# A message-passing layer on one core: a split first group, ten supertiles gathered from 128 rows, a last pass in units of four bins, and an early flag

## The chip, the cores and the metric

The kernel runs on one core of a Trainium2 chip. The core has five engines with an instruction stream each: PE (TensorE, matmuls and weight loads), DVE (VectorE), ACT (ScalarE), POOL (GpSimd) and SP (SyncE, which here only issues DMAs). They share the SBUF and sixteen DMA engines. The metric is device time in microseconds (us) of one execution.

## The reference, cut to what matters

There are N = 12,500 nodes with 128 features and E = 400,000 edges, sorted by `dst`. With `src` as the index to sum over, `dst` as the index to gather from and `rcut` the edge weight, the layer computes:

```
h    = relu(layernorm(x)) @ W_in2f.T                       # 12500 x 128
W    = smu(f_ij @ W_f1.T + b_f1) @ W_f2.T + b_f2           # 400000 x 128, f_ij has 20 columns
msg  = h[dst] * (W * rcut[:, None])                        # one message per edge
agg  = segment_sum(msg, src, 12500)                        # src is random
out  = x + smu(agg @ W_o1.T + b_o1) @ W_o2.T + b_o2
```

`smu` is a smooth activation that the kernel makes of a Gelu and a multiple of its input. `h[dst]` is a gather with neighbouring edges close together; the sum over `src` is a scatter to random rows.

## The kernel before, in words

**Edges.** The edges lie in 3125 tiles of 128. Four tiles are a group (GRP), two groups a supertile (SUP = 8 tiles), so there are 391 supertiles and 782 groups. For each group the main loop makes the messages in this chain: `hide` (PE, L625: filter layer 1), `bend` (ACT, L633: Gelu), `smooth` (DVE, L641), `weigh` (PE, L678: filter layer 2), `gather` (PE, L657 or L659: h[dst] as a product with a one-hot matrix), `take` (ACT, L667: copy out of PSUM), `mix` (DVE, L688), `turn` (PE, L699: four transposes), `send` (ACT, L712 and L715: times the weight, into a message tile `ms`), and `scatter` (POOL, L726): one indirect DMA for each tile of 128 messages, which writes each message into a slot of its own in DRAM. The slot comes from a count: `bins` (DVE, L556, four instructions), `count` (PE, L570 to L573), `read` (DVE, L600) and `number` (DVE, L612). The program order on each engine is written out by hand, and each engine runs its own list in that order.

**One-hot matrix.** Usually the edges of a group look at a window of 42 rows of h, loaded as three bf16 parts (126 partitions); the one-hot `oh` is made on ACT by two instructions a group (`pick_part`, L523 and L524). The first FEW tiles (6 supertiles, so 12 groups) look at the first 128 rows of h instead: `pick` makes the one-hot on DVE (L507), and the gather takes three matmuls (L657) in place of one.

**Epochs and bins.** The nodes are 98 bins of 128. The supertiles are split into ten epochs of 59, 59, 59, 59, 48, 37, 27, 20, 16 and 7. In an epoch every bin has a region of slots in DRAM, of Q blocks of 128 rows (Q is 6 in the first epochs, 2 in the ninth, 1 in the tenth). While an epoch is scattered, `parts` works through the (bin, block) pairs of the epoch before: `fetch` (SP, L757) loads 12 blocks into a tile `rw` (four buffers), `choose` (DVE, L771) makes a selection matrix `se`, `add` (PE, L787) multiplies, and DVE adds the sum to `agg` (L800), 98 x 128 columns. The messages of the last two epochs are made early and kept in DRAM; at the end of the program a short loop only loads and scatters them. In that loop LEFT = 36 of the 196 pairs of the ninth epoch are held back until the last scatter is issued.

**Opening.** Before the loop stands a hand-ordered opening: loads of x, w and the first indices; layernorm and h of the first bin; the one-hot, count and messages of group 0 as a whole; constants in between. `quiet_ends` has POOL clear a tile `zero`, with which the slot regions are cleared by DMA (`clear`, L187 and L191), and fill buffers; it waits for DVE. The list `opening` holds 14 steps (the rest of the first 512 tiles' indices, and h of bins 1 to 3), one of which runs at each of the three `step()` calls of a group. After it come the `steps` that prepare all other nodes and indices, spread over the first epoch by the expression `taken_steps * 3 * (eps_of[0][1] * PER - 15) < slot * COUNT`.

**Last pass.** After the last scatter the rest of the ninth epoch is added, then the tenth: nine fetches of 12 bins (the first of two bins), and for each unit of four bins Gelu (ACT, L1132), a sum (POOL, L1138), the last product (PE, L279), the residual (DVE, L283) and a DMA to `out` (SP, L285). Then a count of violated assumptions (`bad`) is summed over the partitions by a matmul (L1189), loaded by every engine into a register (`values_load`, L1194), and an `If` (L1195) branches over a general path that the inputs do not need. It holds some 270 DMA issues of SP.

Of the kernel before, what the change touches and what calls it, by code (L numbers as in the profile page):

```python
# [9 lines left out]
F32 = mybir.dt.float32  # L10
# [9 lines left out]
P = 128  # L20
# [8 lines left out]
SUP = 8  # L29
# [13 lines left out]
def gnn_kernel(  # L43
# [46 lines left out]
    for a, n in eps_of:  # L90
# [21 lines left out]
    make_identity(nc, ident)  # L112
# [3 lines left out]
    nc.vector.memset(ones1, 1.0)  # L116
# [4 lines left out]
    nc.vector.tensor_scalar(prow, pcol, float(WIN), -float(WIN), op0=ALU.is_ge, op1=ALU.mult)  # L121
    nc.vector.tensor_add(prow, prow, pcol)
    late = const.tile([P, 1], F32, name="late")
    nc.vector.tensor_scalar(late, pcol, float(2 * WIN), -float(WIN), op0=ALU.is_ge, op1=ALU.mult)
    nc.vector.tensor_add(prow, prow, late)
    nrow = const.tile([P, 1], F32, name="nrow")
    nc.vector.tensor_scalar(nrow, prow, -1.0, None, op0=ALU.mult)
    irow = const.tile([P, P], F32, name="irow")
    nc.gpsimd.iota(irow, pattern=[[1, P]], base=0, channel_multiplier=0,
                   allow_small_or_imprecise_dtypes=True)  # L130

# [6 lines left out]
    def counting_constants():  # L138
        nc.vector.tensor_scalar(lift, ident, BIG, None, op0=ALU.mult)
        nc.vector.scalar_tensor_tensor(tri, irow, pcol, lift, op0=ALU.is_gt, op1=ALU.add)  # L140
        nc.vector.memset(ones_h, 1.0)
        nc.vector.tensor_sub(rest_h, ones_h, tri)
        nc.vector.memset(none, 0.0)

    onesb = const.tile([P, P], F32, name="onesb")
    nc.vector.memset(onesb, 1.0)
# [8 lines left out]
    nc.vector.memset(bad, 0.0)  # L155

# [51 lines left out]
    def deviations(a, b):  # L208
        nc.scalar.activation(rstd[:, a:b], mv[:, a:b, 1], AF.Sqrt, bias=eps)
        nc.vector.reciprocal(rstd[:, a:b], rstd[:, a:b])  # L210
        nc.vector.scalar_tensor_tensor(down[:, a:b], mv[:, a:b, 0], -1.0, rstd[:, a:b], op0=ALU.mult, op1=ALU.mult)
# [78 lines left out]
    with tc.tile_pool(name="ld", bufs=4) as ld, \  # L290
# [17 lines left out]
        FEW = 6 * SUP  # L308
# [9 lines left out]
        def whole_bins(to, sf, si):  # L318

            nc.vector.tensor_copy(sf, si)  # L320
            nc.vector.tensor_scalar(to, sf, 1.0 / P, -(P - 1) / (2.0 * P), op0=ALU.mult, op1=ALU.add)
# [81 lines left out]
        nc.sync.dma_start(ds, dst_col[:, 0:FEW])  # L403
        nc.scalar.dma_start(x_sb[:, 0:1, :], bin_rows(x, 0, 1))
        nc.sync.dma_start(ss, src_col[:, 0:FEW])
        nc.scalar.dma_start(w_in, w_in_t)
        fill(0, nc.vector)
        fill(1, nc.vector)
        nc.vector.tensor_copy(irow_ps, irow)
        nc.gpsimd.memset(w_f1, 0.0)  # L410
        nc.sync.dma_start(w_f1[0:R, :], w_f1_t)
        nc.sync.dma_start(w_f1[R:R + 1, :], b_f1)
        nc.sync.dma_start(fbufs[0][0:R, :], f_t[:, 0:SUP * P])
        nc.scalar.dma_start(x_sb[:, 1:HEAD, :], bin_rows(x, 1, HEAD - 1))
        nc.scalar.dma_start(w_o1, w_o1_t)
        nc.sync.dma_start(w_f2, w_f2_t)
        nc.sync.dma_start(b2, b_f2.rearrange("o p -> p o"))
        nc.sync.dma_start(w_sb[:, 0:CH], w_col[:, 0:CH])
        one["fetched"]()
        zr = edge.tile([P, 3 * D], BF, name="zr", bufs=1)  # L420

        def quiet_ends():

            for t in (zero, fbufs[2], zr, fbufs[3], x_sb[:, NB - 1, :]):
                nc.vector.memset(t[:, 0:2], 0.0)  # L425
            nc.gpsimd.memset(zero, 0.0)
            clear(0, len(cleans) - 1, nc.gpsimd)
            fill(2, nc.gpsimd)
            nc.gpsimd.memset(zr, 0.0)
            nc.gpsimd.dma_start(h_dram[NB * P:N + P, :], zr[:N + P - NB * P, :])  # L430
            fill(3, nc.gpsimd)
            nc.gpsimd.memset(x_sb[:, NB - 1, :], 0.0)

        spare = const.tile([P, 2], F32, name="spare")
        nc.scalar.activation(spare[:, 0:1], eps, AF.Sqrt)

# [4 lines left out]
        def later_loads():  # L441
            nc.sync.dma_start(w_o2, w_o2_t)
            nc.sync.dma_start(b1, b_o1.rearrange("o p -> p o"))
# [59 lines left out]
        def pick(s):  # L503

            n = sups[s][1] * P
            oh = edge.tile([P, SUP * P], BF, name="oh", bufs=3)
            nc.vector.tensor_scalar(oh[:, :n], loaded[s][1][:, :n], pcol, None, op0=ALU.is_equal)  # L507
            onehot[s] = oh

        def pick_part(g):  # L510
# [4 lines left out]
            if s < FEW // SUP:  # L515
                if i == 0:
                    pick(s)
                return
# [4 lines left out]
            nc.scalar.activation(oh, loaded[s][1][:, o:o + n], AF.Abs, bias=nrow)  # L523
# [94 lines left out]
        def hide(g):  # L618
# [6 lines left out]
            nc.tensor.matmul(pu[:, :n], w_f1, loaded[g // PER][0][:, o:o + n], start=True, stop=True)  # L625
# [95 lines left out]
        def scatter(g, ms):  # L721

            t, n = groups[g]
            k, ix = epoch[g // PER], taken.pop(g)
            for j in range(n):
# [106 lines left out]
        LEFT = 36  # L832

        def few_bins():
            whole_bins(hi_f[:, 0:FEW], ssf, ss)
# [6 lines left out]
        def spread_group(g):  # L842

            pb = bank("pb")
            for j in range(GRP):
                t = g * GRP + j
                nc.tensor.transpose(pb[:, j, :], dsf[:, t:t + 1].to_broadcast([P, P]), ident)
            return pb.rearrange("p j e -> p (j e)")

        def pick_group(g, pb):  # L850
            nc.vector.tensor_scalar(onehot[0][:, g * GRP * P:(g + 1) * GRP * P], pb, pcol, None, op0=ALU.is_equal)
# [3 lines left out]

        nc.vector.tensor_copy(dsf, ds)
        pb0 = spread_group(0)
        pd = ps1.tile([P, GRP * P], F32, name="pw")
        nc.tensor.transpose(pd[:FEW, 0:P], dsf, ident)
        stats(edge, 0)  # L860
        deviations(0, 1)
        few = edge.tile([FEW, P], BF, name="few", bufs=1)
        nc.scalar.activation(few, pd[:FEW, 0:P], AF.Copy)
        nc.sync.dma_start(rel_dram[0, 0:FEW * P].rearrange("(t e) -> t e", e=P), few)
        few_bins()
# [464 lines left out]
```

## Time and profile before

| | |
|---|---|
| median of 3 runs | 4059.88 us (4059.31 to 4063.59) |
| the profiled execution | 4063.85 us, of which its span from first to last instruction 4062.1 us |
| mean granted TensorE clock | 0.968 |
| busy share of the span | PE 86%, DVE 82%, ACT 73%, POOL 75% |
| scatters (L726) | 3125, first at 19.42 us, last at 3991.16 us |
| last DVE work of a store (L283) ends | 4053.57 us |

All durations below are of the profiled execution, counted from the start of its span. Its own time is 3.97 us above the median. A line such as `L726` is a line of the kernel before. In a group line, `x2944 | 2829.0, 961 | 916.0` is the number of instructions, the busy time, the mean ns of one, and the idle time of the engine just before them. POOL's busy time leaves out what lies between two indirect DMAs.

### The profile page before, as it was taken

How to read it: one execution, taken by the hardware profiler on the slowest of the kernel's cores; microseconds unless marked ns; L12 is line 12 of the kernel's file. 1: busy time of each engine (PE TensorE's matmuls, PEld its weight loads, DVE VectorE, ACT ScalarE, POOL GpSimd, SP SyncE). 2: the span in 40 equal slices, each digit the busy share in tenths (PEclk: the TensorE clock that was granted, in tenths of full speed). 3: DMA queues.
4: the chain of work that ended last, by engine and by line, in shares of the span. 5: the costliest groups of instructions: out<-in, count | busy, mean ns of one | idle time of the engine just before them, and what ended most of it. 6: DMA issues, size and time to landing. Idle time of an engine off the chain costs nothing.

```text
span 4062.1 us, 69847 instructions
## 1 busy us (share of the span) xinstructions
PE 3492.8 (86%) x18417; PEld 2246.9 (55%) x18420; DVE 3328.4 (82%) x7355; ACT 2962.7 (73%) x7256; POOL 3042.2 (75%) x3168
## 2 busy tenths in 40 slices
PE   7777777999988999989999979999899979989657
PEld 3334434555555555555555546666566646656547
DVE  8987776888887888878888878888799869988447
ACT  5779986888886888877888877787777767766001
POOL 6777777777777777777777777777777777777775
PEclk9999998999999999999999999999999989999889
DMA  6976666777756565546565646666566657565987
GB/s 193 240 187 182 190 167 197 210 204 204 208 162 180 174 175 173 173 141 181 174 177 172 176 144 181 182 180 189 154 193 195 183 156 203 170 202 170 274 240 226
DMA packets 510392, 759.72 MB, mean 187 GB/s; under 512 B 174949, under 2 KB 313462, under 8 KB 509856
## 3 DMA queue, kind: packets, MB, share of 16 engines
q1 hardware_dynamic: 402416, 535.77, 48.4%
q0 software_dynamic: 100112, 207.06, 15.3%
q10 hardware_dynamic: 7456, 12.35, 0.8%
q8 instruction: 146, 2.39, 0.3%
q14 instruction: 262, 2.15, 0.2%
HBM read 460.77 MB, written 294.11 MB: 186 GB/s over the span
## 4 chain that ended last, share of the span: by engine, by line
PE 41%; DVE 26%; DMA 13%; ACT 9%; issue 6%; POOL 4%; ACTq 0%; SPq 0%; DVEq 0%; POOLq 0%
PE pw L678 13%; DMA buf<-ms,ix 10%; PE pg L787 10%; DVE se L771 9%; PE pu L625 7%; PE pt L699 7%; DVE mt L688 5%; POOL buf L726 4%; DVE sl L600 3%; ACT ms L715 3%; ACT ge L633 2%; DVE sm L641 2%; PE ph L659 2%; DVE so L556 2%; DVE agg L800 2%
## 5 line engine op out<-in xcount | busy, mean ns | idle before, releaser
L726 POOL DMA_INDIRECT buf<-ms,ix x2944 | 2829.0, 961 | 916.0 <-issue 270.6
L787 PEld LDWEIGHTS pg<-se,rw 128*128 128x128 f32 x8232 | 1080.8, 194 | 343.3 <-issue 277.1
L787 PE MATMUL pg<-se,rw 128*128 128x128 f32 x8232 | 1175.7, 282 | 96.4 <-DVE se L771 75.1
L715 ACT ACTIVATE ms<-pt,w_sb 128x128 f32<-128x128 f32 x3125 | 882.2, 363 | 196.8 <-PE pt L699 176.0
L556 DVE SCALAR_TENSOR_TENSOR so<-irow_ps,hi_f,so 128x98 f16<-128x98 f32 x2936 | 929.7, 317 | 78.0
L678 PE MATMUL pw<-sm,w_f 128*128 128x512 f32 x1564 | 884.1, 648 | 47.9 <-DVE sm L641 46.9
L625 PE MATMUL pu<-f,w_f 128*128 128x512 f32 x1564 | 813.6, 602 | 0.0
L633 ACT ACTIVATE ge<-pu 128x512 f32<-128x512 f32 x782 | 468.0, 598 | 443.6 <-PE pu L625 439.4
L771 DVE TENSOR_TENSOR se<-irow_ps,rw 128x1536 f32<-128x1536 f32 (+2 forms) x356 | 602.3, 1692 | 229.5 <-DMA rw<-buf 228.3
L699 PE MATMUL pt<-ident,mt 128*128 128x128 f32 x2944 | 468.9, 282 | 362.7 <-DVE mt L688 361.1
L688 DVE SCALAR_TENSOR_TENSOR mt<-pw,b,hg 128x512 f32<-128x512 f32 x782 | 583.4, 746 | 173.3 <-ACT hg L667 149.8
L641 DVE SCALAR_TENSOR_TENSOR sm<-pu,ge 128x512 f32<-128x512 f32 x782 | 534.2, 683 | 188.2 <-ACT ge L633 182.4
L699 PEld LDWEIGHTS pt<-ident,mt 128*128 128x128 f32 x2944 | 327.6, 142 | 447.2 <-DVE mt L688 444.4
L524 ACT ACTIVATE oh<-oh,onesb 128x512 bf16<-128x512 bf16 x770 | 555.5, 721 | 25.2
L523 ACT ACTIVATE oh<-rbc,nrow 128x512 bf16<-128x512 bf16 x770 | 551.2, 716 | 1.2 <-DMA rbc<-rel_dram 1.2
L667 ACT ACTIVATE hg<-ph 128x512 f32<-128x512 f32 x782 | 472.1, 604 | 99.9 <-PE ph L659 30.3
L600 DVE TENSOR_REDUCE sl<-pc 128x4 f32<-128x392 f32 x782 | 434.5, 556 | 0.0
L678 PEld LDWEIGHTS pw<-sm,w_f 128*128 128x128 f32 x1564 | 236.5, 191 | 161.8 <-DVE sm L641 124.7
L659 PE MATMUL ph<-oh,hw 126*128 126x512 bf16 x770 | 298.2, 387 | 0.0
L625 PEld LDWEIGHTS pu<-f,w_f 128*128 128x128 f32 x1564 | 256.9, 196 | 67.2 <-issue 57.9
L570 PE MATMUL pc<-so,tri 128*128 128x392 f16 x736 | 243.7, 331 | 1.7 <-DVE agg L425 1.7
L572 PEld LDWEIGHTS <-rest_h 128*128 128x128 f16 x781 | 76.7, 98 | 263.6 <-issue 263.6
(192 smaller groups left out, 2002.1 us busy)
## 6 DMA issues: line engine op xcount, KB each, us to landing
rw<-buf SPq DMA_DIRECT2D x300, 774.0 KB
rbc<-rel_dram SPq DMA_DIRECT2D x389, 256.0 KB
buf<-zero SPq DMA_DIRECT2D x146, 387.0 KB
buf<-ms,ix POOLq DMA_INDIRECT x2944
rw<-buf SPq DMA_DIRECT2D x49, 645.0 KB
f<-in_f_t SPq DMA_DIRECT2D x390, 80.0 KB
hw<-h_dram SPq DMA_DIRECT2D x770, 31.5 KB
kept_rows<-ms ACTq DMA_DIRECT2D x45, 258.0 KB
```

Source lines behind the costliest of these rows:

```text
L524: nc.scalar.activation(oh, oh, AF.Relu, scale=-1.0, bias=onesb[:, 0:1])
L556: nc.vector.scalar_tensor_tensor(so[:, j], irow_ps[:, :NB], hi_f[:, t + j:t + j + 1], so[:, j - 1] if j else before, op0=ALU.is_equal, op1 ...
L600: nc.vector.tensor_reduce(sl[:, :n], pc[:, :n], op=ALU.max, axis=AX.X)
L625: nc.tensor.matmul(pu[:, :n], w_f1, loaded[g // PER][0][:, o:o + n], start=True, stop=True)
L641: nc.vector.scalar_tensor_tensor(sm[:, :n], units_of.pop(g)[:, :n], LIN, hidden[g][:, :n], op0=ALU.mult, op1=ALU.add)
L678: nc.tensor.matmul(pw[:, :n], w_f2, hidden.pop(g)[:, :n], start=True, stop=True)
L688: nc.vector.scalar_tensor_tensor(mt[:, :n], pws.pop(g)[:, :n], b2, rows_of.pop(g)[:, :n], op0=ALU.add, op1=ALU.mult)
L699: nc.tensor.transpose(pt[:, j, :], mt[:, j * P:(j + 1) * P], ident)
L715: nc.scalar.activation(ms[:, j, 0:P], pt[:, j], AF.Copy, scale=w_sb[:, t + j:t + j + 1])
L726: i = nc.gpsimd.indirect_dma_start(out=bufs[k][:, :], out_offset=bass.IndirectOffsetOnAxis(ap=ix[:, j:j + 1], axis=0), in_=ms[:, j, :], in ...
L771: nc.vector.tensor_tensor(se[:, a:a + n], own.unsqueeze(1).to_broadcast([P, n, P]), rows_in[c][:, a:a + n, P:P + 1].to_broadcast([P, n, P] ...
L787: nc.tensor.matmul(pgs[0][:, g, :], rows_in[c][:, o, 0:P], sel[c][:, o, :], start=(q == 0), stop=(q == Q[k] - 1))
```

## The change

1. **First group.** Group 0 is made as its first tile alone (`one_cut`, 128 columns) and then the other three (`others`, 384 columns), each with its own matmuls, Gelu, products and transposes; `scatter_tile` issues the first scatter as soon as the first tile is sent. Eight matmuls on constants (`idle(8)`) stand first on PE.
2. **Early constants and clearing.** The constants of the count are made before the first layernorm; POOL clears `zero` and issues its two DMAs before anything waits for DVE; the row of ones of three of the four `f` buffers comes by DMA instead of a memset. Scaling of w_f2 goes from DVE to ACT, that of w_o1 to a late step.
3. **FEW = 10 supertiles** look at 128 rows, and their one-hot is made on ACT with `pick_part` (bias `pneg`) as for all others; the DVE `pick` goes away.
4. **Opening at half the rate:** 16 steps, one at every second `step()`; the later steps then spread over fewer slots (22 in place of 15).
5. **Last pass** by units of four bins (the last four units are 2, 2, 1 and 1 bins): each is a fetch, a selection, four products, a sum, and its output follows three and four units later. Every third unit's residual goes by ACT and POOL instead of DVE (six units). LEFT is 24.
6. **Flag.** `bad` is summed ahead of the loop of kept scatters, and the register load stands between the ninth epoch's last block and the last pass. The DMA issues of the general path move from SP to ACT.

```diff
-        FEW = 6 * SUP
+        FEW = 10 * SUP
...
+        one_cut, others = (0, P), (P, (GRP - 1) * P)
+        idle(8)
+        stats(edge, 0)
...
+        gather_cut(*one_cut)
+        smooth_cut(*one_cut)
+        take_cut(*one_cut)
+        weigh_cut(*one_cut)
+        hide_cut(*others)
...
+        mix_cut(*one_cut)
+        bend_cut(*others)
+        gather_cut(*others)
+        turn_tile(0)
+        send_tile(0, ix0)
+        smooth_cut(*others)
+        weigh_cut(*others)
+        take_cut(*others)
...
+        for j in range(1, GRP):
+            turn_tile(j)
+            send_tile(j, ix0)
...
-            if s < FEW // SUP:
-                if i == 0:
-                    pick(s)
-                return
-            nc.scalar.activation(oh, loaded[s][1][:, o:o + n], AF.Abs, bias=nrow)
+            nc.scalar.activation(oh, loaded[s][1][:, o:o + n], AF.Abs, bias=pneg if s < FEW // SUP else nrow)
             nc.scalar.activation(oh, oh, AF.Relu, scale=-1.0, bias=onesb[:, 0:1])
...
             if opening:
-                opening.pop(0)()
+                apart_by += 1
+                if apart_by % 2 == 0:
+                    opening.pop(0)()
                 return
...
-        LEFT = 36
+        LEFT = 24
...
+        parts(k - 1, len(work))
+        flag = nc.values_load(nbad[0:1, 0:1], min_val=0, max_val=P * 64)
...
+        for i in range(4 * 3):
+            fetch_unit(i)
+        choose_unit(0)
+        choose_unit(1)
+        for i in range(len(units)):
+            summed_up(i)
+            if i % 3 == 2:
+                for j in range(10, 13):
+                    fetch_unit(i + j)
+            late_one = units[i][1] < GRP
+            if not late_one:
+                bend_unit(i)
+            choose_unit(i + 2)
+            rest_unit(i - 3)
+            store_unit(i - 4)
+            if late_one:
+                bend_unit(i)
+        for i in range(len(units) - 3, len(units) + 1):
+            rest_unit(i)
+            store_unit(i - 1)
...
     with tc.If(flag > 0):
...
-                nc.sync.dma_start(tab[b:b + n, :], zt[:n])
+                nc.scalar.dma_start(tab[b:b + n, :], zt[:n])
```

`summed_up` holds the products and the add to `agg`, `choose_unit` the selection, `bend_unit` the Gelu and the sum, `rest_unit` the last product, `store_unit` the residual and the DMA to `out`.

More of the change, by code (lines that the diff above doesn't have):

```diff
@@ L1064, in gnn_kernel @@
             assert k == 0 or taken_steps == COUNT
[L1066 to L1067 removed]
+        wanted = units
         def homes():
```

349 lines of the change are left out of this document (185 added, 164 removed).

## The prediction

> **What bounds the kernel now.** I read the page's costliest groups first, not its chain: the chain gives PE 41% and POOL 4%, because it hops back through whatever released each short wait. The group of scatters says something else.
>
> ```profile
> L726 POOL DMA_INDIRECT buf<-ms,ix x2944 | 2829.0, 961 | 916.0 <-issue 270.6
> ```
>
> Scatters cost 961 ns and have 311 ns of idle time before each (916.0/2944). POOL's timeline shows that these 0.30 us are there even when nothing is waited for, so a scatter costs 1.264 us. The 3125 scatters run from 19.42 to 3991.16: 3124 x 1.264 = 3948.7 of 3971.7 us. Real waits are 23.0 us in all. So POOL's queue of scatters bounds the middle, whatever PE or DVE do there, and the time is: start of the queue + 3948.7 + waits + what follows the last scatter. The change touches the two ends. The start, in POOL's timeline:
>
> ```profile
> 15.61 0.22 POOL L432 MEMSET agg<- 128x128 f32 x1
> 19.42 1.05 POOL L726 DMA_INDIRECT buf<-ms,ix  x1 [3.59 <-ACT ge L633]
> ...
> 25.42 0.96 POOL L726 DMA_INDIRECT buf<-ms,ix  x1 [1.10 <-ACT ms L715]
> 26.68 0.96 POOL L726 DMA_INDIRECT buf<-ms,ix  x1 [0.30 <-DVE so L556]
> ...
> 64.21 0.96 POOL L726 DMA_INDIRECT buf<-ms,ix  x1 [3.17 <-ACT ms L715]
> ...
> 81.24 0.96 POOL L726 DMA_INDIRECT buf<-ms,ix  x1 [1.83 <-ACT ms L715]
> ```
>
> Idle time above 0.30 is a starved queue: at groups 1, 8 and 11. What counts is therefore the effective start, a scatter's time less 1.264 for each scatter before it: 19.42 for group 0, 20.37 at 25.42 (scatter 4), 23.77 at 64.21 (32), 25.63 at 81.24 (44). After that messages are ahead (ms of group 39 is ready 13 us early), and the remaining lost time, mostly at 2450 and 2640 us, lies where the change does nothing. The PE clock in this stage, from the windows (PE, weight loads, DVE, ACT, POOL, then clock, DMA share, GB/s):
>
> ```profile
> 9.60:13.00 3.40, 1.44 (x8) 0.58 (x7) 2.88 (x17) 1.66 (x6) 1.55 (x2) 1.00 0.00 0
> 13.00:19.80 6.80, 5.45 (x11) 2.06 (x11) 3.53 (x9) 2.19 (x7) 3.21 (x7) 0.50 0.75 225
> ```
>
> Group 0 is made at half clock: the two passes of L678 take 2.04 us there and 1.13 later. The end, in windows and in the instructions of the branch:
>
> ```profile
> 4000.00:4010.00 10.00, 5.39 (x39) 4.65 (x40) 8.10 (x13) 2.82 (x5) 2.91 (x4) 1.00 1.08 263
> 4010.00:4050.00 40.00, 38.63 (x340) 37.90 (x338) 35.72 (x49) 14.96 (x21) 26.95 (x22) 1.00 0.74 211
> 4050.00:4053.60 3.60, 2.47 (x19) 2.16 (x18) 2.23 (x6) 0.51 (x1) 1.68 (x3) 1.00 0.60 182
> ```
>
> ```profile
> L1194 DVEq TENSOR_LOAD <-nbad x1: 792/792/792, 4053.7 to 4053.7; - x1
> L1195 SPq EVENT_SEMAPHORE  x8: 17/17/17, 4057.5 to 4060.4; - x8
> L1195 POOLq INC_SWDGE_SEM  x1: 1255/1255/1255, 4054.8 to 4054.8; - x1
> L1195 SPq COMPARE_BRANCH  x1: 53/53/53, 4054.8 to 4054.8; - x1
> L1195 PEldq EVENT_SEMAPHORE  x1: 51/51/51, 4058.3 to 4058.3; - x1
> ```
>
> The last pass is PE's: 97% busy over 40 us, 54% while it starts. Then 8.5 us pass from the last store's sum (4053.57) to the end (4062.09): the flag's load (0.8), a branch after which SP's next instruction comes 2.6 us later, and SP's waits up to 4060.4.
>
> **The change, part by part.**
>
> *First scatter.* The layernorm of bin 0 keeps its place (rstd near 4.5 us: x lands no sooner, and the constants moved ahead of it on DVE, about 1.6 us of short rows, fill the wait that the second buffer fill and index rows filled). Eight 128-column matmuls are 16 passes of 0.25 us (L625's cold 1.99 for eight such pieces), 2.0 to 6.1 us, so the first transpose waits until near 7. Then come shorn, table load (1.28), parts of h, the first tile's chain. Taking rows scaled to 128 columns I get its scatter at 14.3 us at full clock and 15.6 at half. POOL's clear, issued near 2.5 instead of 13.03, is no longer in its way. Tiles 1 to 3 need Gelu, sum, product and transposes again at 384 columns: 16.3 or 18.1 us, so POOL idles about 1 to 2 us between.
>
> *Group 1.* ACT now has, between its sends: Gelu 0.60, four one-hot instructions 4 x 0.72, copy 0.60, Gelu 0.60, two more one-hot, bins 0.20: 6.3 us in line, where group 0's sends end at 16.9 (full clock) or 18.6. Group 1's scatter starts at 24.4 to 26.0; I take 24.9, so an effective start of 19.8. Here most of the first tile's 4 to 5 us is lost again: the queue runs dry before group 1.
>
> The rule "TensorE: Matmul & The Clock Gate", Part 1, of the Trainium skill speaks against the eight matmuls: a window of about 3.4 us of activity frees the clock, and an idle one takes it back, so warming PE ahead of waits buys nothing; by it alone the half-clock end would hold, group 1 at 26.0 and 1.1 us less gain. The 0.50 above, in a stretch where PE was 80% busy, agrees that the clock is easily lost.
>
> *Groups 1 to 19.* The opening's steps come at half rate. ACT per group: 0.60 + 0.60 + 0.20 + 1.14 + two one-hot 1.43 = 4.0, plus about 0.35 of opening; PE: 0.66 + 1.13 + 0.81 (three matmuls) + 1.02 + 0.83 = 4.45. The queue takes 5.06. Before, groups 1 to 7 came every 4.75 us (sends at 24.78 and 53.26); I take 4.6, a lead of 4.6 us at group 11. Then the heavy steps begin that before began at group 5: there groups 7 to 11 took 27.4 us (53.26 to 80.61) against 20.2 of the queue, a loss of 7.1. Lead 4.6 against loss 7.1 leaves a wait of 2.5: effective start 22.3, against 25.63. **Gain 3.3.** Bounds: no new wait, group 1 at 24.4: 6.3; a pace as over groups 1 to 11 before, 5.58, kept to group 19: 3 lost. The second is far off, since in it the opening ran at full rate.
>
> *Steps over fewer slots, moved constants, w_o1 late:* 7% denser steps in a stretch with a lead of up to 18 us: nothing.
>
> *LEFT 24 and the ninth epoch's rest.* PE was ahead of the list when the last scatter went (28 of the 36 held pairs left, done at 3999.9, paced by fetches). Twelve pairs earlier help only as far as fetches arrive: 0 to 1 us, taken as 0.
>
> *Last pass.* PE's work is unchanged: 392 passes at 0.111 (0.89 for eight) = 43.7 us. Before it took 4000.9 to 4052.9, 8.3 idle: 4.6 in the start, 2.2 in the middle, 1.5 at the end. After, with four-bin fetches and selections (0.69 on DVE instead of 1.75 for twelve), the start costs one selection and three units paced by DVE at 1.25 instead of 0.45: 2.4, the middle 2, the end 1.8. DVE's rows: selections 23 x 0.32/3 dearer, six residuals of 0.69 fewer: 1.6 per unit against PE's 1.78. POOL: 1.28 per unit, 2.56 in every third: 1.71, close. SP: 18 more issues of 0.36, beside PE. The early register load costs 0 to 0.8 on DVE ahead of the first selection, 0.4 taken. **Gain 8.3 - 6.2 + 0.4 (smaller first selection) = 2.5**, bounds 0 and 5.
>
> "DMA: Bandwidth & Descriptors", Bandwidth, of the Trainium skill advises transfers of 1 MiB and more, giving 138 GB/s for 64 KB and 341 for 1 MB; a unit's 264 KB at the lower rate would take 1.9 us, an estimate, and pace the pass 3 us slower. No row here isolates one such fetch; the last pass as a whole moved 211 GB/s.
>
> *End.* The flag's 0.8 is gone from here; SP no longer skips some 270 issues but seven instructions, like ACT before, which went on within 0.2 us. Late next are PE and DVE, whose jumps took 3.7 and 3.0. With 1.6 for the final barrier: 3.2 + 1.6 = 4.8 after the last store against 8.5, less the 0.4 above: **gain 3.3**, bounds 0.8 (SP fetches anyway) and 4. ACT's jump becomes long, but starts some 2 us earlier.
>
> Sum 3.3 + 2.5 + 3.3 = 9.1: 4063.85 becomes 4054.7 in a profiled execution, and the median 4059.88 becomes **4050.8**.
>
> **Rivals.** *Ends only:* the queue's effective start stays at 25.6, because heavy steps run it dry whenever they start; gain 5.8 or less, 4054 to 4058. For it: the wait at 81.24 fixed the start before, not the first scatter. *Both ends go well:* no wait after group 1 and a pass without gaps, 6.3 + 5 + 4: 4044.6. *Slower:* the three-matmul gathers and ACT one-hots of groups 12 to 19 meet the heavy steps, and all groups to 19 come at 6.07 us, the pace of groups 4 to 11 before (38.14 to 80.61). Group 19 is then ready at 24.3 + 18 x 6.07 = 133.6, an effective start of 38: 12 later, less 5.8 at the end: 4066. It decides from a pace of about 5.6. Against it: from group 12 on, with ACT one-hots and steps, sends came every 4.56 us (84.85 to 121.31). *The change does not do what it says:* SP still waits 2.5 us for code after the branch, and PE idles as before: 4056.
>
> **How the numbers follow.** Forecast (about 4047 to 4052.5) 0.45; both ends well 0.12; ends only 0.20; nothing at the end 0.10; slower 0.13. 0.2% is 8.1 us, about what a measurement tells from no change. The forecast straddles that line: nearly all of it and of the good case, 0.56, is faster; 0.32 lies within; of the slower case and its milder forms 0.12 is beyond. The range takes in the good case to 4043 and the end-only cases to 4059.
>
> **What would show it.** First scatter at 14 to 16 us, a gap of 1 to 2 us behind it, group 1 at 24 to 26; idle time over 0.30 between groups 11 and 20 of 2 to 3 us in sum; scatter 44 near 78; last scatter near 3988. PE over 90% busy from 5 us after its first tenth-epoch product. From last L283-like sum to the end about 5 us, SP without a gap after its branch. The forecast is wrong if the idle time before group 1 is over 7 us, if scatters starve past group 30, or if SP's first wait after the branch still comes 2.6 us late.

## The result and the profile after

The changed kernel takes **4109.03 us** (median of 4 runs, 4102.37 to 4110.1), the kernel before beside it 4059.6 us: a ratio of 1.0117, with a 95% interval of 1.0105 to 1.0129. It is slower by 1.2%, clear of the spread of the runs, and 50 us above the upper end of the range that was given. Its profiled span is 4108.2 us against 4062.1. The 46.1 us between them lie as follows: the last scatter leaves at 4048.94 instead of 3991.16 us (+57.8), the last store ends 53.3 us after it instead of 62.4 (-9.1), and the end comes 5.94 us after that instead of 8.51 (-2.6). So both ends came out shorter, and the middle, to which the prediction gave no change, lost 58 us.

The scatters in the page of the changed kernel: as many, and as long, but with 72 us more of idle time before them.

```profile
L725 POOL DMA_INDIRECT buf<-ms,ix x2944 | 2826.6, 960 | 988.0 <-issue 282.3
```

POOL's timeline of the changed kernel, where the opening was shown before. The bracket is the idle time and what ended it:

```profile
14.78 1.04 POOL L725 DMA_INDIRECT buf<-ms,ix  x1 [10.89 <-ACT ms L895]
17.57 0.97 POOL L725 DMA_INDIRECT buf<-ms,ix  x1 [1.75 <-ACT ms L895]
...
29.14 0.96 POOL L725 DMA_INDIRECT buf<-ms,ix  x1 [8.08 <-ACT ms L710]
...
34.54 0.96 POOL L725 DMA_INDIRECT buf<-ms,ix  x1 [0.60 <-ACT ms L710]
```

The first scatter comes 4.6 us sooner, as forecast, and 8 us of idle time before group 1 give it back. The effective start (a scatter's time less 1.264 us for each scatter before it) is 24.1 us at group 1 and still 24.8 at group 11, where the kernel before had 25.6. From there on it falls behind, for as long as the first epoch lasts: 27.1 at group 20, 36.0 at group 40, 71.9 at group 128, where the kernel before has 26.0, 26.9 and 29.5. In the waits of POOL from 83 to 640 us (us in total, times, longest) the message tile is what is late:

```profile
POOL buf L725 <- ACT ms L710: 65.9, 93, 4.2
```

The kernel before has 28.0 us in 92 waits on that line there, none over 0.3: that is the 0.3 us that stand before every scatter. Two views say what is behind it. The first is the windows from 85 to 650 us, where TensorE has nothing of an epoch before to add up, and from 650 to 3900 us. The columns are PE, weight loads, DVE, ACT and POOL busy, each with its number of instructions, then granted clock, DMA share and GB/s. The kernel before:

```profile
85.00:650.00 565.00, 416.61 (x1672) 211.28 (x1671) 441.69 (x1203) 471.91 (x1180) 429.75 (x444) 0.94 0.71 192
650.00:3900.00 3250.00, 2906.76 (x15695) 1905.16 (x15694) 2721.61 (x5834) 2426.40 (x5931) 2459.11 (x2562) 0.98 0.63 184
```

The kernel after:

```profile
85.00:650.00 565.00, 492.39 (x1578) 215.14 (x1579) 422.07 (x1147) 447.74 (x1106) 398.61 (x411) 0.80 0.62 182
650.00:3900.00 3250.00, 3042.62 (x15529) 1858.85 (x15528) 2721.75 (x5863) 2435.72 (x5983) 2443.39 (x2551) 0.98 0.60 182
```

PE is busy for 76 us more in the first stretch and gets fewer instructions done; the clock falls from 0.94 to 0.80. In the second it is busy for 136 us more at the same clock. The other engines do about the same or less. The second view is PE's timeline at full clock late in the kernel, at the first layer of the filter. The kernel before:

```profile
2347.87 0.61 PE L787 MATMUL pg<-se,rw 128*128 128x128 f32 x4
2348.32 1.02 PE L625 MATMUL pu<-f,w_f 128*128 128x512 f32 x2
2349.18 0.33 PE L570 MATMUL pc<-so,tri 128*128 128x392 f16 x1
```

The kernel after:

```profile
2346.74 0.61 PE L786 MATMUL pg<-se,rw 128*128 128x128 f32 x4
2347.28 1.12 PE L620 MATMUL pu<-f,w_f 21*128 21x512 f32 x2
2348.33 0.34 PE L565 MATMUL pc<-so,tri 128*128 128x392 f16 x1
```

The shapes tell the edit that the prediction did not see. Neither the list of the six parts of the change nor the excerpt of the diff shown with it has it; the whole diff has it in `hide`, and the new `hide_cut` is written the same way:

```diff
-            nc.tensor.matmul(pu[:, :n], w_f1, loaded[g // PER][0][:, o:o + n], start=True, stop=True)
+            nc.tensor.matmul(pu[:, :n], w_f1[:R + 1], loaded[g // PER][0][:R + 1, o:o + n], start=True, stop=True)
```

The first layer multiplies 21 rows instead of 128, 107 of which were zeros in the weights. From the same four products of `add`, the same matmul of `count` starts 1.59 us later (2348.33 less 2346.74) instead of 1.31. One by one, the median distances from the matmul before `hide` to its first pass, to its second, and to the next matmul are 0.20, 0.53 and 0.52 us, where 128 rows have 0.11, 0.43 and 0.43. In the sum this is 0.28 us a group of TensorE (medians of 1.26 and 0.97). The weight loads (PEld) at the same place show where it lies. The kernel before:

```profile
2348.21 0.30 PEld L625 LDWEIGHTS pu<-f,w_f 128*128 128x128 f32 x2
2348.75 0.10 PEld L570 LDWEIGHTS <-tri 128*128 128x128 f16 x1 [0.24 <-issue]
```

The kernel after:

```profile
2347.28 0.29 PEld L620 LDWEIGHTS pu<-f,w_f 21*128 21x128 f32 x2
2348.33 0.10 PEld L565 LDWEIGHTS <-tri 128*128 128x128 f16 x1 [0.76 <-issue]
```

Before, the weights of `hide` begin to load 0.11 us ahead of its first pass, and those of `count` 0.43 us ahead of its matmul, beside the work in front of them. After, both loads begin with their own matmul.

The end, in the same windows as before, and at the branch:

```profile
4050.00:4060.00 10.00, 7.76 (x66) 7.28 (x65) 7.22 (x13) 1.44 (x2) 1.58 (x2) 1.00 0.87 227
4060.00:4099.00 39.00, 39.00 (x351) 39.00 (x351) 35.41 (x63) 19.09 (x29) 34.04 (x28) 1.00 0.88 241
4099.00:4102.30 3.30, 2.24 (x16) 1.63 (x14) 3.23 (x11) 0.77 (x2) 0.00 (x0) 1.00 0.79 238
```

```profile
L1268 SPq EVENT_SEMAPHORE  x8: 17/17/17, 4105.3 to 4106.5; - x8
...
L1268 PEldq COMPARE_BRANCH  x1: 4242/4242/4242, 4101.2 to 4101.2; - x1
...
L1268 SPq COMPARE_BRANCH  x1: 53/53/53, 4105.1 to 4105.1; - x1
```

PE has no idle time left in the 39 us of the last pass, and SP goes on 0.2 us behind its branch instead of 2.6. What holds SP now is its own issue of the last stores, up to 4105.1. In e1 below, SP's first wait behind the branch comes 1.0 us after it.

### The profile page after: what moved, and what is told of

Same layout as the page of the kernel before. It is cut to its first block, busy times and chain, and to the rows that moved or that the text cites. A ratio compares the mean times of both kernels' runs of the same rounds, so it can differ in the third digit from the quotient of the medians.

```text
span 4108.2 us, 69958 instructions
## 1 busy us (share of the span) xinstructions
PE 3757.8 (91%) x18454; PEld 2245.5 (55%) x18459; DVE 3332.9 (81%) x7360; ACT 2974.3 (72%) x7286; POOL 3041.5 (74%) x3166
## 4 chain that ended last, share of the span: by engine, by line
PE 61%; DVE 20%; ACT 6%; DMA 5%; issue 4%; POOL 3%; ACTq 0%; DVEq 0%; SPq 0%; POOLq 0%
PE pw L673 16%; PE pg L786 14%; PE pu L620 13%; PE pt L694 8%; DVE se L770 7%; DVE mt L683 4%; DMA buf<-ms,ix 3%; POOL buf L725 3%; PE ph L654 3%; PE pc L565 3%; DVE sl L595 2%; DVE sm L636 2%; ACT ge L628 2%; ACT ms L710 2%; PE pc L567 1%
## 5 line engine op out<-in xcount | busy, mean ns | idle before, releaser
L786 PEld LDWEIGHTS pg<-se,rw 128*128 128x128 f32 x8036 | 1058.2, 194 | 332.7 <-issue 275.6
L786 PE MATMUL pg<-se,rw 128*128 128x128 f32 x8036 | 1150.1, 283 | 86.7 <-DVE se L770 76.9
L673 PE MATMUL pw<-sm,w_f 128*128 128x512 f32 x1562 | 897.8, 658 | 39.9 <-DVE sm L636 37.8
L620 PE MATMUL pu<-f,w_f 21*128 21x512 f32 x1562 | 905.5, 660 | 0.0
L770 DVE TENSOR_TENSOR se<-irow_ps,rw 128x1536 f32<-128x1536 f32 (+1 forms) x345 | 587.8, 1704 | 166.9 <-DMA rw<-buf 165.3
L694 PE MATMUL pt<-ident,mt 128*128 128x128 f32 x2940 | 477.9, 287 | 181.3 <-DVE mt L683 173.2
L519 ACT ACTIVATE oh<-oh,onesb 128x512 bf16<-128x512 bf16 x780 | 562.8, 721 | 25.6
L694 PEld LDWEIGHTS pt<-ident,mt 128*128 128x128 f32 x2940 | 340.2, 145 | 246.8 <-DVE mt L683 239.3
L565 PEld LDWEIGHTS <-tri 128*128 128x128 f16 x782 | 75.0, 96 | 615.2 <-issue 599.2
L620 PEld LDWEIGHTS pu<-f,w_f 21*128 21x128 f32 x1562 | 236.3, 189 | 207.2 <-issue 122.8
L565 PE MATMUL pc<-so,tri 128*128 128x392 f16 x736 | 255.3, 347 | 0.0
```

The source lines that it names most:

```text
L519: nc.scalar.activation(oh, oh, AF.Relu, scale=-1.0, bias=onesb[:, 0:1])
L620: nc.tensor.matmul(pu[:, :n], w_f1[:R + 1], loaded[g // PER][0][:R + 1, o:o + n], start=True, stop=True)
L673: nc.tensor.matmul(pw[:, :n], w_f2, hidden.pop(g)[:, :n], start=True, stop=True)
L694: nc.tensor.transpose(pt[:, j, :], mt[:, j * P:(j + 1) * P], ident)
L770: nc.vector.tensor_tensor(se[:, a:a + n], own.unsqueeze(1).to_broadcast([P, n, P]), rows_in[c][:, a:a + n, P:P + 1].to_broadcast([P, n, P] ...
L786: nc.tensor.matmul(pgs[0][:, g, :], rows_in[c][:, o, 0:P], sel[c][:, o, :], start=(q == 0), stop=(q == Q[k] - 1))
```

## The experiments

Two theories stood against each other for most of this, and both turned out to be part of it: that `hide` on few rows brings the granted clock down (*idle rows*), and that its weight loads stop overlapping (*the gap*). "Half clock" is the time that the profile records at granted clock 0.5 in the first 650 us, and "starved" is POOL's idle time before scatters beyond 0.31 us each. Ratios are to the kernel before, run beside each experiment, with the 95% interval. Eight of the runs (e5 to e8 and e13 to e16) went to two chips on which the kernel before itself takes 5219 and 5321 us and every kernel starves all along; their times are compared with each other alone. Half clock and starved time come from one profiled execution of each kernel.

**e1: the change with `hide` on 128 rows.**

```diff
-            nc.tensor.matmul(pu[:, :n], w_f1[:R + 1], loaded[g // PER][0][:R + 1, o:o + n], start=True, stop=True)
+            nc.tensor.matmul(pu[:, :n], w_f1[:128], loaded[g // PER][0][:128, o:o + n], start=True, stop=True)
```

The same goes for `hide_cut`; w_f1 is zeroed, and whole buffers of ones are written on POOL instead of the row by DMA.

> The changed kernel with the first filter product (hide and hide_cut) on all 128 rows of f and w_f1, as in the kernel before, in place of 21; the unused rows are ones in f and zeros in w_f1, filled on POOL, and the three one-row DMAs go. Theory rows (a product on 21 of 128 rows does not count as full activity of PE, so its clock is halved all through the first epoch, which makes the message chain longer than the scatter queue's 5.06 us a group): clock halved for under 100 us in the first 650 us (after: 239), scatter queue starved for under 15 us (after: 88 in all), time 4059.6 - 12 (end) - 3 (start) = about 4045. Theory opening (128-row gathers on ACT for 20 groups, opening at half rate, denser steps): time stays near 4109, the queue still starves for over 60 us.

4051.25 us, ratio 0.9978 (0.9969 to 0.9987): the whole loss is gone. Half clock 99 us (after: 225), starved in the first 650 us 6.5 (50.7).

```profile
85.00:650.00 565.00, 425.02 (x1686) 215.13 (x1686) 445.86 (x1210) 470.60 (x1175) 429.04 (x443) 0.92 0.70 195
650.00:3900.00 3250.00, 2914.15 (x15715) 1911.65 (x15714) 2725.47 (x5836) 2421.91 (x5924) 2455.78 (x2563) 0.98 0.63 185
```

**e2: the kernel before with `hide` on 21 rows, and nothing else.**

> The kernel before with nothing changed but the first filter product on 21 rows in place of 128. Theory rows: halved clock for over 180 us of the first 650 us (before: 82), scatters starved for 40 to 70 us more, time 4100 to 4125. Theory opening: 4059 to 4062, nothing but a product on fewer rows, at the same 1.02 us.

4111.86 us, ratio 1.0126 (1.0111 to 1.0142); half clock 212 us, 82 in the kernel before. The edit alone makes the loss, in either kernel.

**e3: the change with `hide` on 64 rows.**

> As e1, but the first filter product on 64 rows. Theory rows, if activity counts rows in use: between after and e1, halved clock 100 to 200 us in the first 650 us, 4060 to 4095; if there is a threshold instead: equal to one of the two. Theory opening: 4109 as e1.

4092.95 us, ratio 1.0081 (1.0066 to 1.0096), half clock 144.5 us. It was read at first as a dose of idle rows. That reading does not hold: 64 rows have the whole gap too (0.20, 0.53, 0.52).

**e4: the change with FEW at 6 supertiles and an opening step at every call.**

> The changed kernel (21 rows) with FEW back at 6 supertiles, the opening at one step at each call and the later steps over 15 fewer slots as before; the one-hot stays on ACT. Theory rows: 4100 to 4115, the clock still halved. Theory opening: the starving goes, 4045 to 4060.

4108.85 us, ratio 1.0120 (1.0101 to 1.0138). The pace of the opening and the three-matmul gathers, the prediction's own mechanism for a slower kernel, are not it. Its one-hot matrices stay on ACT; that these are not it either is seen in e2, which has the old ones.

**e5 and e9: 21 rows, and full matmuls beside them.** In the first epoch:

```diff
+            for _ in range(3 if g < 118 else 0):
+                nc.tensor.matmul(pu.rearrange("p (j e) -> p j e", j=GRP), onesw,
+                                 onesw.unsqueeze(1).to_broadcast([P, GRP, P]), start=True, stop=True)
             nc.tensor.matmul(pu[:, :n], w_f1[:R + 1], loaded[g // PER][0][:R + 1, o:o + n], start=True, stop=True)
```

> The changed kernel, its hide still on 21 rows, with three matmuls of 128 rows by 512 bfloat16 columns added ahead of each group's hide for groups 1 to 117, into the same PSUM tile, which the hide then writes over. Theory (the granted clock falls because the array's rows stand idle): more work on TensorE, about 0.2 us a matmul at full clock or 0.6 us a group, makes the kernel faster: half clock in the first 650 us falls from 225 us to under 150, the starved time of the scatters in them from 51 us to under 30, and the time to between 4060 and 4090 us. Rival (the message chain is too long for another reason, and the clock only follows from it): 0.6 us more in each group's chain; the time is 4109 us or more, up to 4109 + 117 x 0.6 = 4179 us.

On a chip with 5219 us before: 5335 us, ratio 1.0244 (1.0185 to 1.0302), half clock 188 us. It tells nothing of the size, so it was repeated.

> The same kernel as e5 (the changed kernel with hide on 21 rows, and three full 128-row bfloat16 matmuls ahead of each hide for groups 1 to 117), for a chip on which the kernel before takes about 4060 us; where e5 ran it took 5219 us, and every stage was slower. Theory (idle rows bring the granted clock down): half clock in the first 650 us under 150 us, where the changed kernel had 225, and a time of 4060 to 4095 us. Rival (the length of the chain, with the clock only following): 4109 us or more. A third way, which e5 brings up (2.4% slower than before, with 188 us of half clock in the first 650 us): the clock answers to the kind of work and not to the rows alone, half clock stays above 180 us, and the time is 4109 to 4150 us.

4127.32 us, ratio 1.0158 (1.0138 to 1.0179), with half clock at 92 us. The clock is back to that of 128 rows and the time is not: neither theory had that.

```profile
85.00:650.00 565.00, 488.71 (x1876) 214.87 (x1878) 420.89 (x1143) 442.35 (x1103) 397.52 (x409) 0.93 0.68 183
```

PE is busy for 489 us here as in the changed kernel (492), 92 us of them in the added matmuls, and the scatters starve as long (54.2 against 50.7 us). Two things follow. A starved chain is not enough to bring the clock down: here it is starved at a good clock. And what the scatters feel fits TensorE's time for a group, whether the clock stretches it or added work does.

**e6 and e10: 128 rows, and two full matmuls beside them in the first epoch.**

> The changed kernel with hide back on 128 rows (4051.25 us when it ran alone), and two matmuls of 128 rows by 512 bfloat16 columns added ahead of each group's hide for groups 1 to 117. Theory (idle rows bring the clock down): little is left to win, since the scatters starve for 6.5 us in the first 650 us there, of which about 2 could go with half clock under 60 us instead of 99: 4046 to 4052 us. Rival (TensorE's time per group is what the scatters wait for): 0.4 us more a group in the groups that have no room, slower: 4055 us or more.

Ratio 1.0016 (0.9992 to 1.004) on that chip, half clock 150 us against 198 without the two.

> The same kernel as e6 (hide on 128 rows, two full bfloat16 matmuls ahead of each hide for groups 1 to 117), for a chip on which the kernel before takes about 4060 us. Theory: half clock in the first 650 us under 99 us, and 4046 to 4052 us. Rival: 0.4 us more a group where there is no room, 4055 us or more. e6 had less half clock in those 650 us than the same kernel without the two matmuls (150 us against 198) and no better time.

4062.02 us, ratio 1.0000 (0.9991 to 1.001). Half clock falls to 67 us, and yet it is 0.2% slower than e1, starved for 17.5 us instead of 6.5. From the matmul before `hide` to the one behind it 1.60 us pass in the mean instead of 1.20 (120 to 640 us): 0.4 us a group cost 11 us there.

**e7: e1 without the eight idle matmuls.**

> The changed kernel with hide on 128 rows, without the eight idle matmuls at its start. Theory of the prediction (the idle matmuls buy nothing): first scatter at 16.0 us plus or minus 0.3, group 1 at 26.4 plus or minus 0.5, time within 2 us of 4051.25. Rival (they bring the full clock for some microseconds of the head): the first 15 us are at half clock throughout, the first scatter comes 0.6 to 1.5 us later, at 16.6 to 17.5 us, and the time is 1 us longer or so.

First scatter 16.17 us, and 16.16 in e8 on the same chip, which has them; group 1 at 26.86 and 27.34. They buy nothing here. In the changed kernel itself, TensorE has no full clock before 25.3 us, in spite of them. They stand in e5 too, which has full clock from 5.3 to 12.2 us and its first scatter at 12.49 us, 2.3 us sooner than the changed kernel, but group 1 at 29.84: what they bring differs between profiled executions, and group 1, which has added matmuls in e5, keeps none of it.

**e8, e11 and e12: e1 with LEFT at 36, and at 12.**

> The changed kernel with hide on 128 rows and LEFT back at 36, as before the change. Theory (part of the gain of the last pass comes from the twelve products of the ninth epoch that run ahead of the last messages): the ninth epoch is done 2 us later after the last scatter than the 6.7 us with LEFT at 24, and the stretch from the last scatter to the last store is 56.5 to 57.5 us instead of 54.9. Rival (the units of four bins alone make the gain): the stretch stays at 54.5 to 55.3 us.

The ninth epoch is done 27.1 us after the last scatter, 19.5 in e7 with LEFT at 24, and the stretch to the last store takes 75.3 against 67.7: the direction of the theory, on a chip where all stretches are longer.

> The same kernel as e8 (hide on 128 rows, LEFT at 36 as before the change), for a chip on which the kernel before takes about 4060 us. Theory (the twelve products of the ninth epoch that run ahead of the last messages are part of the gain of the last pass): the ninth epoch is done at 8.7 to 9.5 us after the last scatter where LEFT at 24 had 6.7, and the stretch from last scatter to last store is 56.5 to 57.5 us instead of 54.9. Rival (the units of four bins alone): 54.5 to 55.3 us.

4053.73 us, ratio 0.9977 (0.9967 to 0.9987); the ninth epoch done at 8.2, the stretch 56.4 us: just under the theory's figures, over the rival's.

> The changed kernel with hide on 128 rows and LEFT at 12 in place of 24. Theory (products of the ninth epoch that run ahead of the last messages shorten the last pass for as long as TensorE has room): the ninth epoch is done 2 us sooner after the last scatter than 6.7 us, the last scatter moves by under 0.5 us, and the time is 2 us under that of hide on 128 rows, 4048 to 4050 us. Rival (the last messages wait behind the products): the last scatter comes 2 us later or more, and the time is 4051 us or more.

4050.40 us, ratio 0.9968 (0.9956 to 0.9981); the ninth epoch done at 10.7, the stretch 58.9, with half clock for its first 7 us in the profiled run, and the last scatter 2.4 us later than in e1, on another chip. Theory and rival each miss a part of that. By time, LEFT at 36, 24 and 12 can't be told apart (0.9977, 0.9978, 0.9968). What LEFT is worth stays open, at 0 to 2 us. With e1 these are the versions that beat both kernels most clearly.

**e13 and e14: 21 rows from group 118 on alone, and up to it alone.**

```diff
+            K = P if g < 118 else R + 1
+            nc.tensor.matmul(pu[:, :n], w_f1[:K], loaded[g // PER][0][:K, o:o + n], start=True, stop=True)
```

> The changed kernel with hide on 128 rows for groups 1 to 117 and on 21 rows from group 118 on. Theory (the gap in the weight loads costs 0.28 us a group at full clock, and late in the kernel the clock does not differ): the first 650 us are as with 128 rows, starved for 6 to 8 us; past them the starved time is 25 to 45 us, as in the kernels on 21 rows, where 128 rows have 11 to 14; 4063 to 4085 us. Rival (the loss is the clock of the first epoch alone): 4050 to 4054 us.

> The changed kernel with hide on 21 rows for groups 0 to 117 and on 128 rows from group 118 on. Theory: starved for 40 to 52 us in the first 650 us, with 200 us or more of half clock, and for 11 to 16 us past them: 4085 to 4098 us. Rival (what is lost late follows from the lateness of the first epoch, not from the rows): over 20 us past 650 us, 4100 us or more.

On a chip with 5321 us before: e13 1.0185 (1.0103 to 1.0266), e14 0.9977 (0.9937 to 1.0017). There the 21 rows cost in the long part behind the first epoch. This does not single out the gap: past 650 us e13 has 1466 us of half clock and e14, on 128 rows there, 1119, while on the other chips the two kinds do not differ in it (changed kernel 168 us, e1 188). In the first epoch no loss shows there, against what was expected of e14, although half clock goes to 341 us (e13, on 128 rows: 191). All four kernels of that chip starve for over 130 us in it, and the interval of e14, 21 us to either side, would hide a loss of the 15 us that the other chips leave for the first epoch.

**e15 and e17: `hide` on 72 rows. e16 and e18: 128 rows, and a tiny matmul on 21 rows ahead.**

```diff
+            nc.tensor.matmul(pu[:, 0:16], onesw[:R + 1], onesw[:R + 1, 0:16], start=True, stop=True)
             nc.tensor.matmul(pu[:, :n], w_f1[:128], loaded[g // PER][0][:128, o:o + n], start=True, stop=True)
```

> The changed kernel with hide on 72 rows. Theory of the gap (a weight load on more than 64 rows overlaps again, and the idle rows themselves cost nothing): hide's two matmuls start 0.43 us apart at full clock, half clock in the first 650 us is 80 to 110 us, and the time is 4050 to 4056 us. Rival (idle rows bring the clock down, whatever the loads do): half clock 130 us or more there, as with 64 rows (144 us), and 4070 to 4093 us.

> The changed kernel with hide on 128 rows, and ahead of each hide one bfloat16 matmul on 21 rows and 16 columns, into the same PSUM tile. Theory of the gap: a load on 21 rows waits for the matmul before it, and the next load for this one, some 0.2 to 0.3 us a group at full clock, twice that at half; half clock in the first 650 us rises with it to 120 us or more, starved time there to 15 us or more: 4065 to 4105 us. Rival (rows idle during hide itself bring the clock down; a gap of 0.2 us costs what e10's 0.45 us of extra work a group cost, or less): half clock 80 to 105 us, and 4051 to 4062 us.

On the chip of e13: e15 1.0008 (0.9977 to 1.0038), e16 1.0179 (1.0119 to 1.0239). The two effects come apart. 72 rows have no gap (0.11, 0.43, 0.43) and half clock of 222 us; the tiny matmul makes the gap (1.28 us from the matmul before to the one behind, instead of 0.97) and leaves half clock at 188, where e13 on the same chip has 191 with 128 rows and no gap. So the gap does not make the half clock; the idle rows do. PE's timeline with 72 rows, from e17 below:

```profile
2345.98 1.02 PE L621 MATMUL pu<-f,w_f 72*128 72x512 f32 x2
2346.84 0.33 PE L566 MATMUL pc<-so,tri 128*128 128x392 f16 x1
```

From `hide` to `count` 0.86 us pass, as on 128 rows (2348.32 to 2349.18), in place of 1.05 on 21 rows.

> The same kernel as e15 (hide on 72 rows: rows idle and no gap), for a chip on which the kernel before takes about 4060 us. Theory (gap and clock each have a share; TensorE's time per group is what the scatters wait for): half clock in the first 650 us 100 to 130 us against 99 with 128 rows, and 4051 to 4060 us. Rival (the idle rows carry most of the loss): 4070 us or more.

4061.79 us, ratio 0.9987 (0.9978 to 0.9997), half clock 143 us, starved 12.4 in the first 650 us and 11.7 behind it: idle rows without the gap cost some 4 us against e1, with intervals that overlap.

```profile
85.00:650.00 565.00, 435.46 (x1656) 218.04 (x1655) 439.85 (x1194) 464.92 (x1160) 428.21 (x442) 0.89 0.69 195
650.00:3900.00 3250.00, 2906.16 (x15672) 1898.99 (x15673) 2721.43 (x5842) 2428.22 (x5937) 2459.10 (x2559) 0.98 0.63 184
```

> The same kernel as e16 (hide on 128 rows, a tiny 21-row matmul ahead of it: the gap alone, 0.31 us a group), for a chip on which the kernel before takes about 4060 us. Theory: starved 12 to 17 us in the first 650 us, since 0.40 us more a group brought 17.5 us in e10, and 25 to 35 us past them, where the kernels on 21 rows have 29 to 43 and 128 rows 12.6: 4070 to 4085 us, a third to a half of the loss of 58 us against 128 rows. Rival (the clock carries the loss, the gap little): under 8 us and under 15 us, 4051 to 4058 us.

4098.77 us, ratio 1.0079 (1.0062 to 1.0096), half clock 78.5 us, starved 9.9 in the first 650 us and 47.6 behind it.

```profile
85.00:650.00 565.00, 448.47 (x1758) 211.92 (x1757) 440.50 (x1193) 464.15 (x1158) 428.46 (x440) 0.93 0.70 194
650.00:3900.00 3250.00, 3059.39 (x16182) 1975.48 (x16180) 2708.66 (x5825) 2411.92 (x5933) 2431.59 (x2531) 0.99 0.62 181
```

PE's timeline of e18 at the same place:

```profile
2349.92 0.61 PE L790 MATMUL pg<-se,rw 128*128 128x128 f32 x4
2350.46 0.18 PE L623 MATMUL pu<-onesw 21*128 21x16 bf16 x1
2350.57 1.13 PE L624 MATMUL pu<-f,w_f 128*128 128x512 f32 x2
2351.53 0.33 PE L568 MATMUL pc<-so,tri 128*128 128x392 f16 x1
```

Sixteen columns cost 0.3 us: the distance from the four products of `add` to `count` is 1.61 us, as with 21 rows in `hide` itself. PE is busy for 145 us more than in e1 from 650 to 3900 us, as in the changed kernel (128), at the best clock of all. The gap alone, with the tiny matmul that makes it, is worth 1.0079 - 0.9978 = 1.0% or 41 us, more than was expected (4070 to 4085), of the 1.0117 - 0.9978 = 1.4% or 56 us that the 21 rows cost. The rest is lost in the first epoch, where the two add up to TensorE's time:

| kernel | gap | half clock | PE busy, 85 to 650 us | starved, first 650 us | starved, later |
|---|---|---|---|---|---|
| before, 128 rows | no | 82 | 417 | 5.3 | 10.4 |
| e1, 128 rows | no | 99 | 425 | 6.5 | 12.6 |
| e17, 72 rows | no | 143 | 435 | 12.4 | 11.7 |
| e18, 128 rows and tiny | yes | 79 | 448 | 9.9 | 47.6 |
| e10, 128 rows and full ones | no | 67 | 451 | 17.5 | 11.3 |
| e3, 64 rows | yes | 144 | 465 | 26.1 | 30.1 |
| after, 21 rows | yes | 225 | 492 | 50.7 | 29.0 |
| e9, 21 rows and full ones | yes | 92 | 489 | 54.2 | 43.2 |
| e2, before on 21 rows | yes | 212 | 495 | 29.7 | 41.8 |
| e4, after with the old opening | yes | 229 | 498 | 40.7 | 35.3 |

The starved time of the first epoch rises with PE's busy time there, whatever makes it: 5 to 12 us up to 435 of 565 us, 30 to 54 us at 489 to 498, where the kernels differ among themselves for a reason that was not sought. That of the later part is 10 to 14 us without the gap and 29 to 48 with it. No run adds other work of 0.3 us a group there, so that it is the gap as such, and not any 0.3 us of TensorE, is not shown; e10, where 0.4 us of added work a group costs 11 us in the first epoch, speaks for any.

How it reaches the scatters can be read from the program order and the trace. Between groups 118 and 532 the loop also makes the 46 groups of the last two epochs, whose messages are only kept: TensorE has to make ten groups in the time that the queue takes for nine, 4.55 us each instead of 5.06. In this stretch PE is busy for 94% of 650 to 2750 us in the changed kernel and 91% in e1, and a group's first message is ready 4.8 us ahead of its scatter in the mean instead of 9.1 (groups 120 to 530). Behind 2800 us, where nothing is made for later, the changed kernel, e1 and e18 do not starve at all, e3 for 0.5 us and e9 for 4.4.

## Why the prediction was wrong

**The failed step** is the reading of the diff ahead of the sum. The prediction carries `hide` at "1.02", the row of 128 rows, in its PE sum of groups 1 to 19, and holds POOL's queue to bound the middle "whatever PE or DVE do there". The edit that puts `hide` on 21 rows stands in the whole diff and was passed over, so that its two terms are missing from the sum: 0.28 us of TensorE in each of 781 groups, and the clock of the first epoch (at half for 225 us instead of 99 in e1). Together they put the last scatter 62.9 us later (4048.94 against 3986.06 in e1), 2.7 of them by group 1. A rule that could have raised it stands in the Trainium skill, "TensorEngine Tiling (Array Packing)", Key Properties: a change of tiling mode drains TensorE, and that page of the Trainium skill has modes of 32, 64 and 128 rows. It does not say that a plain matmul on fewer rows changes the mode. The trace fits that reading: 21 and 64 rows have the gap of 0.28 us, 72 rows do not.

"Whatever PE does" failed as well. PE at 86% was not on the path on average, but its room in the first epoch was under 0.4 us a group (e10: 11 us more of starving), and in the later part 145 us more in 3250 (e18 against e1) brought 35 us more of starving.

**What it said would show it wrong** did: idle time before group 1 over 7 us (8.08), and scatters starved past group 30. The third sign, a late first wait of SP behind the branch, did not come (0.2 us). The rival on the slower side got the place half right (the first epoch's pace) and the mechanism wrong: e4 has the old opening and the same loss, e2 has nothing of the change but the 21 rows and the same loss, and between groups 1 and 11 the changed kernel lost 0.7 us.

**The rest of the sum is tested by e1**, where the 21 rows are undone: 4051.25 us, with 4050.8 predicted. Its terms:

- *First scatter* (14.3 to 15.6): 14.78 in the changed kernel, 16.02 in e1. Tile 1 (16.3 or 18.1): 17.57 and 18.04. Right for the changed kernel; in e1, which fills three whole buffers and w_f1 on POOL, 0.4 us over the range.
- *Group 1* (24.9, up to 26.0): 26.45 in e1, 29.14 in the changed kernel, in which TensorE is at half clock to 25.3 us; `hide` of group 1 takes 2.07 us at 18.68, and that of group 2 takes 1.12 at 25.40. Missed, for the changed kernel by the same overlooked edit. The eight idle matmuls bought nothing (e7: 16.17 us without them, 16.16 with). The prediction had read this out of the Trainium skill, "TensorE: Matmul & The Clock Gate", Part 1, and the half-clock end that it gave for it, 26.0, was the nearer one.
- *Groups 1 to 19* (gain 3.3, effective start 22.3): 22.7 at group 20 in e1, against 26.0 before. Right in size, though by another way: the loss of 7.1 us at the heavy steps did not come, and group 1 was later.
- *Last pass* (gain 2.5, bounds 0 and 5): mis-sized. The stretch from last scatter to last store fell by 7.5 us in e1 and 9.1 in the changed kernel. From the first product of the tenth epoch to PE's last of the pass, 52.2 us became 46.0 in the changed kernel and in e1: 6.2 us, over the bound of 5. Against the 43.7 us of work that the prediction counted, 2.3 us of idle time are left where it left 6.2. The rule on transfers in the Trainium skill, "DMA: Bandwidth & Descriptors", Bandwidth, which the prediction priced at 3 us against, did not bite: 241 GB/s in the 39 us of the pass, with PE never idle.
- *LEFT and the ninth epoch* (0 to 1, taken as 0): the ninth epoch was done at 6.7 us (e1) and 5.1 (after) instead of 8.8, where LEFT at 36 has 8.2: 0 to 2, not settled.
- *End* (gain 3.3): 2.6 in the changed kernel, 2.8 in e1. SP's branch went as forecast in the changed kernel; what the sum lacked is one late `out` issue on SP that took 1.73 us (1.40 in e1), where the others took 0.4 to 0.6.
- *The sum* (9.1): e1's profiled span is 15.4 us under that of the kernel before (5.1 at the last scatter, 7.5 and 2.8 behind it), the medians are 8.4 apart (4059.66 and 4051.25), since one profiled execution lay 4.2 us above its median and the other 2.8 below. That forecast and e1 lie 0.5 us apart is therefore in part luck: the terms gave 6.3 us too little (1.8 at the start, 5.0 in the last pass with the ninth epoch, 0.5 too much at the end), and the profiled executions stand 7.0 further apart than the medians.

## What to carry to other kernels

Read a diff for shapes before anything else: a matmul that is cut to its useful rows does the same work in the same passes, and can cost more, in the load that no longer overlaps and in the clock. Leave zeros in the weights rather than cutting rows, unless the trace shows that neither the distance from start to start nor the clock changes: here 72 rows kept the distance and 64 did not, and both lowered the clock. An engine beside the critical queue still has a limit per unit of work: compare its time for a group, in the stage with the worst clock, with the queue's pace, and not its share of the whole span.

## What the runs showed of the hardware that was not expected

- A two-pass float32 matmul on 21 or 64 rows between matmuls on 128 costs 0.28 us of TensorE at full clock (1.26 against 0.97 us from the matmul before to the one behind, for two passes), one of 16 columns 0.31 us; 72 rows have the distances of 128.
- Rows that stand idle bring the granted clock down, without the gap too: half clock in the first 650 us is 99 us with 128 rows, 143 with 72 (no gap), 225 with 21 (gap), and 92 with 21 when full matmuls on constant ones run beside them. In the kernel before, e1, e11, e12 and e18, all with `hide` on 128 rows, it is 79 to 99. The 128-row matmul that avoids it has zeros in 107 rows of its weights and ones in its moving rows: rows in use count here, although their weights are zero.
- The same program took 4060 us on some chips and 5219 or 5321 us on two others, there with a granted clock of 0.88 instead of 0.97 and PE at 75 to 76% of three windows in which it is at 91 to 98% elsewhere. The cause was not looked for.
